# Two attention layers on one core: layer 0's maxima from VectorE to GpSimd, projections in pieces of 256 columns taken in two rounds, and GpSimd's side pieces only where VectorE has its own

## The chip, the cores and the metric

The kernel runs on one core of one Trainium2 chip. The core has five engines with instruction queues of their own: TensorE (PE; its weight loads are listed apart as PEld), VectorE (DVE), ScalarE (ACT), GpSimd (POOL) and SyncE (SP), which here only issues DMAs. The metric is the time of one execution on the device, in microseconds (us), as the median of several runs. The profile is that of one further execution.

## The reference

The inputs are `x` (3327 x 128) and a 0/1 adjacency `adj` (3327 x 3327, ones on the diagonal). Two layers follow each other, each with a residual and a layer norm. Layer 0 is one graph attention over the 3327 nodes. Layer 1 reshapes q, k and v to (128, 3327, 8): it is 128 separate attentions over all 3327 x 3327 pairs, each with inner length 8, and the adjacency is added twice to the scores.

```python
# layer 0
H = X @ W.T + b;  s = H @ a_s;  r = H @ a_r
e = leaky_relu(A * s + A * r.T, 0.2)
att = softmax(where(A > 0, e, NEG), axis=1);  H_out = att @ H
x = layernorm(x + H_out)
# layer 1, d = 128, n = 3327, h = 8
q = (x @ Wq.T).reshape(d, n, h)      # k and v alike
a = einsum('dnh,dmh->dnm', q, k) * d ** -0.5 + adj + adj
a = softmax(a, axis=2)
out = einsum('dnm,dmh->dnh', a, v).reshape(n, h * d)
x = layernorm(x + out @ Wo.T)
```

## The kernel before, in words

**Layer 1 sets the frame.** The 128 attentions are taken four at a time: 32 *groups*. In each group the 3327 queries are cut into seven *blocks* of columns (six of 476, the last of 472), and in each block the 3327 keys into 26 *chunks* of 128 rows. The loop walks groups, blocks and then 26 *rounds* per block, numbered n = 0 to 25; a round computes the scores of two half-chunks (a half-chunk is one chunk for two of the four attentions, 128 x 952 values). Three chunks make a *stretch* of three rounds; the ninth stretch of a block has only two chunks and two rounds, n = 24 and 25.

In a round TensorE first writes the scores of the two half-chunks into PSUM (`scb`, L154). What follows depends on the chunk:

- Every third chunk (0, 3, 6 ... 24, called `times`): ScalarE takes the exponential straight from PSUM (L1136, 128 x 952), and GpSimd multiplies it by a factor made from the adjacency (L1137).
- The other chunks: VectorE adds the adjacency to the scores (L1139, 128 x 952), and ScalarE takes the exponential one or two rounds later, mostly for the whole chunk at once (L968, 128 x 1904; `late`, `exp_late`).

Four rounds after a chunk is complete (`LAG = 4`), `products` multiplies it on TensorE with the values and adds it to the block's sums (`av`, L938). TensorE works through its queue in order, so a product that waits holds back the scores behind it. After the last chunk VectorE copies the sums out (L948). In the first group the factors are not there yet: for each of its 63 stretches GpSimd makes one from the adjacency (`make_factor`, L782) and a DMA stores it for the later groups.

**Layer 0 and the projections are spread over the rounds as side work.** Only the first tile of 128 rows is computed ahead of the loop; the other 25 tiles (`layer0(t)`) are cut into pieces, which `work_tensor` and `work` place in the rounds. A tile of layer 0 needs, for each of 26 chunks of neighbours, a maximum of a row and a column vector (`weigh`, L310, 128 x 129), a product with the adjacency (`mask`, L319, three chunks at once, 128 x 384), and a matmul (`product`, through L243). Then come a chain of small VectorE operations, a transpose, and the projections to k, q and v: `project` computes 128 columns into a PSUM bank, `halves` writes them as an upper part `hi` (L405) and the remainder `lo` (L408), `values` copies v out (L429). VectorE also counts the adjacency's entries (`count`, L328), and finished tiles of layer 1 are projected and normalised by `result`.

Each piece has a kind: "p" for TensorE, "d" for VectorE, "m" for GpSimd, "x" for a load that takes no place. Two rows of pieces wait for places, `main` (products, chain, projections, results) and `aside` (maxima, masks, counts); each is taken strictly in its order. A "d" piece is allowed in ten rounds of a block, n = 0, 4, 7, 10, 13, 16, 19, 22, 24 and 25, one piece each (`lane`); these ten are called *places* below. A "p" piece is allowed at n = 3 and at the same rounds but 0. An "m" piece is allowed in every round, one each. In `work` the pieces come behind the round's own additions and multiplications on their engines.

A tile has to be ready 18 rounds before the end of the group ahead of its first reader (`OPEN`, `reads`). If it is not, `finish_to` issues what is missing at once, without regard to places.

Of the kernel before, what the change touches and what calls it, by code (L numbers as in the profile page):

```python
# [13 lines left out]
ALU = mybir.AluOpType  # L14
# [7 lines left out]
LOWEST = -3.0e38  # L22
# [25 lines left out]
def kernel(  # L48
# [27 lines left out]
    nc = tc.nc  # L76
# [75 lines left out]
    def special():  # L152
# [9 lines left out]
        with ExitStack() as sx, tc.manual_schedule(engines=ALL):  # L162
# [8 lines left out]
            T3 = P // 3 + 1  # L171
# [97 lines left out]
            def layer0(t, side=True, trow=None, bank=bank, held=None):  # L269
# [5 lines left out]
                s = {"a": {}, "w": {}}  # L275
# [25 lines left out]
                def weigh(n, c0, c1):  # L301
                    i0 = CH[n][0]
                    if c0 == i0:
                        s["w"][n] = bgw.tile([P, CW, 3 * T3], F32, name="w")
                    for i in range(c0, c1):
                        w, e = s["w"][n][:, i - i0, :r], er[:, i : i + 1]
                        if side:

                            w = s["w"][n][:, i - i0, :].rearrange("p (a b) -> p a b", b=T3)
                            nc.vector.tensor_scalar(w, s["t"][:, :, :T3], e, None, op0=ALU.max)  # L310
                        else:
                            nc.vector.scalar_tensor_tensor(
                                w, trow[:, :r], e, s["a"][n][:, i - i0, :r], op0=ALU.max, op1=ALU.mult
                            )

                def mask(n, c0, c1):
                    i0 = CH[n][0]
                    w = s["w"][n][:, c0 - i0 : c1 - i0, :r]
                    nc.gpsimd.tensor_tensor(w, w, s["a"][n][:, c0 - i0 : c1 - i0, :r], op=ALU.mult)  # L319

                def count(n, h, k):
                    c = CH[n][1] - CH[n][0]
                    c0, c1 = c * h // 3, c * (h + 1) // 3
                    if c1 > c0:
                        a = s["a"][n][:, c0:c1, :r]
                        z = bg1.tile([P, (CW + 2) // 3, P], BF16, name="dump")[:, : c1 - c0, :r]
                        at = 6 * n + 2 * h + k
                        nc.vector.tensor_scalar(  # L328
                            z, a, float(k), None, op0=ALU.is_equal, op1=ALU.add, accum_out=even[:, t, at : at + 1]
                        )  # L330
# [56 lines left out]
                chain += [("d", together(*root[10:], scale)), ("p", turn), ("d", keep_turned)]  # L387


                QW = 128 if side else 512  # L390

                def project(w, c):
                    s["b"] = bank()
                    (by_columns if side else whole)(
                        s["b"][:, :QW], s["xT"], w[:, c : c + QW], r, start=True, stop=True
                    )

                def halves(dst, c, scale):
                    if c % 512 == 0:
                        s["hi"] = bg2.tile([P, 512], F32R, name="hi")  # L400
                        s["lo"] = bg2.tile([P, 512], F32R, name="lo")
                    o = c % 512
                    hi, lo = s["hi"], s["lo"]
                    if side:
                        nc.vector.tensor_scalar(hi[:r, o : o + QW], s["b"][:r, :QW], scale, None, op0=ALU.mult)  # L405
                    else:
                        nc.scalar.mul(hi[:r, o : o + QW], s["b"][:r, :QW], scale)
                    nc.vector.scalar_tensor_tensor(  # L408
                        lo[:r, o : o + QW], s["b"][:r, :QW], scale, hi[:r, o : o + QW].bitcast(F32),
                        op0=ALU.mult, op1=ALU.subtract,  # L410
                    )
                    if o + QW == 512:
                        h0 = c // 512 * 4
                        for half, sb in ((0, hi), (1, lo)):
                            at = (h0 * 2 + half if dst is qT else half * H + h0) * G + t * P * D
                            for p0, p1 in _cut(r):
                                later = held.append if held is not None and dst is qT else issue
                                engine = nc.sync if later is issue else nc.scalar
                                later(
                                    lambda at=at, sb=sb, p0=p0, p1=p1, engine=engine: engine.dma_start(  # L420
                                        _ap(dst, at + p0 * D, [[D, p1 - p0], [2 * G if dst is qT else G, 4], [1, D]]),
                                        sb[p0:p1].bitcast(F32).rearrange("p (h c) -> p h c", c=D),
                                    )
                                )
# [18 lines left out]
                for w, dst, sc in ((wk, kT, 1.0), (wq, qT, half_scale)):  # L443
                    for c in range(0, H * D, QW):
                        chain += [
                            ("p", lambda w=w, c=c: project(w, c)),
                            ("d", lambda dst=dst, c=c, sc=sc: halves(dst, c, sc)),
                        ]
                for c in range(0, H * D, QW):
                    chain += [("p", lambda c=c: project(wv, c)), ("d", lambda c=c: values(c))]  # L450
# [1 line left out]
                main, aside = [("x", load)], [("r", load_row)] if side else []  # L452
# [10 lines left out]
                for n, (i0, i1) in enumerate(CH):  # L463

                    aside.append(("n", ("P", q0 + n - 2, 0)))
                    for c0 in range(i0, i1, 3):
                        c1 = min(c0 + 3, i1)
                        aside.append(("d", lambda n=n, c0=c0, c1=min(c0 + 2, c1): weigh(n, c0, c1)))
                        if c0 + 2 < c1:
                            aside.append(("d", lambda n=n, c0=c0 + 2, c1=c1: weigh(n, c0, c1)))  # L470
                        if side:
                            aside.append(("m", lambda n=n, c0=c0, c1=c1: mask(n, c0, c1)))
                    aside.append(("t", ("W", q0 + n)))
                    c = [("d", lambda n=n, h=h, k=k: count(n, h, k)) for h in range(3) for k in range(2)]
                    counts.append(c)
                    main.append(("n", ("W", q0 + n, 3)))
                    if i1 == NT:
                        main.append(("m", biased))
                    main += [("p", lambda i=i: product(i)) for i in range(i0, i1)] + [("t", ("P", q0 + n))]
                    aside.append(counts[-1])  # L480
# [446 lines left out]
            NR = len(rounds)  # L927
# [56 lines left out]
            def lane(kind, n):  # L984
                middle = n % 3 == 1 and 4 <= n < NR - 2
                if kind == "p":
                    return int(middle or n == 3 or n >= NR - 2)
                return int(middle or n == 0 or n >= NR - 2)

            made = [layer0(t) for t in range(1, NT)]  # L990
# [2 lines left out]
            aside = []  # L993
# [25 lines left out]
            side = {"main": [], "aside": aside, "since": {"main": 0, "aside": 0}, "read": -2}  # L1019
# [27 lines left out]
            def run(row, now):  # L1047
                side[row].pop(0)[1]()
                side["since"][row] = now
# [6 lines left out]
                    run("main", now)  # L1056

            def work(now, n):
                room, pool = lane("d", n), 1
                for row in ("main", "aside"):  # L1060
                    while True:
                        kind = head(row, now)
                        if kind == "x":
                            pass
                        elif kind == "d" and room:
                            room -= 1
                            if row == "main":
                                side["read"] = now
                        elif kind == "m" and pool:
                            pool -= 1  # L1070
                        else:
                            break
                        run(row, now)
# [21 lines left out]
            for g in range(NG):  # L1095
                k4, v4, _ = group
                for b in range(NBLK):
                    s = Block()
                    s.g, s.b, s.q4, s.k4, s.v4, s.left, s.e, added = g, b, queries[0], k4, v4, NT, {}, {}
                    w = s.w = exact[b][2]  # L1100
                    for n, rnd in enumerate(rounds):
                        at = b * NR + n
                        if n in starts:
                            m = (g * NBLK + b) * NST + starts[n]
# [16 lines left out]
                        sc = []  # L1121
# [18 lines left out]
                        now = g * total + at  # L1140
# [403 lines left out]
```

## Time and profile before

| | |
|---|---|
| median of 3 runs | 10001.89 us (9998.2 to 10005.2) |
| the profiled execution's own time | 10004.91 us |
| its span | 10003.1 us |
| ACT busy | 9892.4 us (99%) |
| PE busy | 9461.4 us (95%) |
| DVE busy | 9334.1 us (93%) |
| POOL busy | 9201.7 us (92%) |
| first to last exponential of layer 1 | 65.9 to 9977.8 us |

The span leaves out 1.8 us of the profiled execution's time. Busy times are unions of the instructions' intervals. A duration in a row runs from an instruction's start to its end, and on DVE, ACT and POOL two neighbours overlap by 0.03 to 0.2 us when neither waits, so that the sum of the durations is above the busy time, and what one more instruction takes from its engine is somewhat less than its duration. "Idle before" is the time in which the engine stood still ahead of an instruction, with what ended it.

### The profile page before, as it was taken

The page shows a single profiled execution, that of the slowest core. Times are in us where ns is not written, and L with a number is a line of the kernel's source. Part 1 is how long each engine was busy: PE and PEld are TensorE (multiplying, and loading weights), DVE is VectorE, ACT ScalarE, POOL GpSimd, SP SyncE. Part 2 cuts the span into 40 slices and gives each one's busy share as a digit, 9 for nine tenths or more (in the row PEclk, how much of TensorE's full clock was granted, in tenths as well). Part 3 has the DMA queues.
Part 4 walks back from the last instruction along what each step waited for, and adds up shares of the span by engine and source line. Part 5 has one row for each costly group of instructions (what it writes and reads, how often), then busy time and mean ns, then how long its engine had stood idle before and what let it go on. Part 6 is the DMA issues. An engine that isn't in the chain of part 4 may idle for free.

```text
span 10003.1 us, 212173 instructions
## 1 busy us (share of the span) xinstructions
PE 9461.4 (95%) x81923; PEld 3078.5 (31%) x81923; DVE 9334.1 (93%) x11592; ACT 9892.4 (99%) x8352; POOL 9201.7 (92%) x4416
## 2 busy tenths in 40 slices
PE   7999999999999999999999999999999999999998
PEld 2233333333233333323333332333332333332222
DVE  7999999999999999999999999999999999999998
ACT  7999999999999999999999999999999999999998
POOL 7999999999999999999999999999999999999998
PEclk9999999999999999999999999999999999999999
DMA  7665666655656656656566665566665566656554
GB/s 200 200 176 169 177 172 177 178 167 174 177 165 175 182 161 178 177 169 176 165 173 174 181 179 164 163 178 179 177 174 168 164 179 177 175 161 171 167 168 125
DMA packets 1383200, 1728.31 MB, mean 173 GB/s; under 512 B 347463, under 2 KB 1370657, under 8 KB 1378079
## 3 DMA queue, kind: packets, MB, share of 16 engines
q1 hardware_dynamic: 1371828, 1712.03, 60.1%
q8 instruction: 644, 10.55, 0.4%
q10 hardware_dynamic: 10347, 2.61, 0.1%
q14 instruction: 381, 3.12, 0.1%
HBM read 1610.23 MB, written 103.93 MB: 171 GB/s over the span
## 4 chain that ended last, share of the span: by engine, by line
ACT 40%; PE 24%; POOL 16%; issue 11%; DVE 6%; DMA 2%; SPq 1%; POOLq 0%; ACTq 0%; DVEq 0%
ACT e L968 25%; POOL e L1137 16%; ACT e L1136 15%; PE scb L154 12%; PE av L938 11%; DVE e L1139 4%; PE bank L243 1%; DVE o L948 1%; DVE lo L408 0%; DMA q4b<-qT 0%; POOL w L319 0%; DMA at<-ftd 0%; DVE hi L405 0%; DMA k4b<-kT 0%; DVE w L310 0%
## 5 line engine op out<-in xcount | busy, mean ns | idle before, releaser
L1137 POOL TENSOR_TENSOR e<-e,at 128x952 f32<-128x952 f32 (+1 forms) x4032 | 8956.7, 2237 | 718.9 <-ACT e L1136 641.7
L1139 DVE TENSOR_TENSOR e<-scb,at 128x952 f32<-128x952 f32 (+1 forms) x7616 | 8420.0, 1143 | 579.3 <-PE scb L154 477.8
L968 ACT ACTIVATE e<-e 128x1904 f32<-128x1904 f32 (+2 forms) x4256 | 7104.0, 1678 | 2.0 <-DVE e L1139 1.6
L938 PE MATMUL av<-e,v4b 128*32 128x476 f32 x46592 | 5917.6, 572 | 60.6 <-DVE o L948 41.9
L154 PE MATMUL scb<-q4b,k4b 32*128 32x476 f32 (+1 forms) x23296 | 3749.2, 486 | 442.8 <-ACT e L1136 370.8
L1136 ACT ACTIVATE e<-scb 128x952 f32<-128x952 f32 (+1 forms) x4032 | 4078.6, 1012 | 57.5 <-PE scb L154 33.8
L154 PEld LDWEIGHTS scb<-q4b,k4b 32*128 32x128 f32 (+1 forms) x23296 | 1764.2, 189 | 5371.8 <-ACT e L1136 3489.9
L938 PEld LDWEIGHTS av<-e,v4b 128*32 128x32 f32 x46592 | 1059.2, 108 | 1140.0 <-issue 933.0
L243 PE MATMUL bank<-hsb,w 128*32 128x129 f32 (+1 forms) x5200 | 277.8, 285 | 0.0
L328 DVE TENSOR_SCALAR_CACHE_REDUCE dump<-a 128x384 bf16<-128x384 f32 (+2 forms) x468 | 247.1, 528 | 0.6
L319 POOL TENSOR_TENSOR w<-w,a 128x384 f32<-128x384 f32 (+3 forms) x225 | 207.7, 923 | 0.1
L310 DVE TENSOR_SCALAR w<-trow,er 128x129 f32<-128x129 f32 x650 | 201.1, 338 | 0.0
L948 DVE COPY o<-av 128x476 f32<-128x476 f32 (+1 forms) x224 | 145.9, 651 | 8.1 <-PE av L938 7.2
L243 PEld LDWEIGHTS bank<-hsb,w 128*32 128x32 f32 (+1 forms) x5200 | 102.4, 108 | 148.0 <-issue 148.0
L408 DVE SCALAR_TENSOR_TENSOR lo<-bank,hi 128x128 fp32r<-128x128 f32 (+1 forms) x400 | 116.5, 291 | 13.8
L405 DVE TENSOR_SCALAR hi<-bank 128x128 fp32r<-128x128 f32 (+1 forms) x400 | 112.0, 280 | 0.0
L243 PE MATMUL bank<-wv,x1T 128*32 128x128 f32 x1600 | 85.6, 286 | 3.9 <-DVE vb L429 3.9
L243 PE MATMUL bank<-wq,x1T 128*32 128x128 f32 x1600 | 85.4, 285 | 0.0
L243 PE MATMUL bank<-wk,x1T 128*32 128x128 f32 x1600 | 85.4, 285 | 0.0
L243 PE MATMUL bank<-wo,ot 128*32 128x128 f32 x1600 | 85.2, 285 | 0.0
L429 DVE COPY vb<-bank 128x128 f32<-128x128 f32 (+1 forms) x200 | 56.1, 281 | 5.8 <-PE bank L243 5.8
L503 PE MATMUL bank<-ident,o 128*128 128x128 f32 x225 | 52.0, 304 | 0.0
(123 smaller groups left out, 659.7 us busy)
## 6 DMA issues: line engine op xcount, KB each, us to landing
at<-in_adjT_dram SPq DMA_DIRECT2D x1536, 476.0 KB
at<-ftd SPq DMA_DIRECT2D x1674, 238.0 KB
at<-in_adjT_dram SPq DMA_DIRECT2D x256, 472.0 KB
at<-ftd SPq DMA_DIRECT2D x279, 236.0 KB
k4b<-kT SPq DMA_DIRECT2D x128, 415.9 KB
q4b<-qT SPq DMA_DIRECT2D x1528, 29.8 KB
at<-in_adjT_dram SPq DMA_DIRECT2D x186, 208.2 KB
a<-in_adjT_dram SPq DMA_DIRECT2D x50, 504.0 KB
```

What stands on the lines that cost most here:

```text
L154: nc.tensor.matmul(dst, k4[32 * j : 32 * j + H4, first_key(i) : first_key(i) + 2 * r - 1 : 2], q4[32 * j : 32 * j + H4, :nb], start=True, ...
L243: nc.tensor.matmul(dst[c0:c1], w[:, c0:c1], mov, **kw)
L310: nc.vector.tensor_scalar(w, s["t"][:, :, :T3], e, None, op0=ALU.max)
L319: nc.gpsimd.tensor_tensor(w, w, s["a"][n][:, c0 - i0 : c1 - i0, :r], op=ALU.mult)
L328: nc.vector.tensor_scalar(z, a, float(k), None, op0=ALU.is_equal, op1=ALU.add, accum_out=even[:, t, at : at + 1])
L408: nc.vector.scalar_tensor_tensor(lo[:r, o : o + QW], s["b"][:r, :QW], scale, hi[:r, o : o + QW].bitcast(F32), op0=ALU.mult, op1=ALU.subtract,)
L938: nc.tensor.matmul(s.av[32 * j : 32 * j + 32, : s.w], s.v4[:r, j, i * H1 : i * H1 + 32], e[:r, j, : s.w], start=(s.left == NT - 1), stop=( ...
L948: nc.vector.tensor_copy(o4[:, :w], s.av[:, :w])
L968: nc.scalar.activation(e, e, AF.Exp, scale=2.0)
L1136: nc.scalar.activation(eh, z[:r, :, :w], AF.Exp, scale=2.0)
L1137: nc.gpsimd.tensor_tensor(eh, eh, ah, op=ALU.mult)
L1139: nc.vector.tensor_tensor(eh, z[:r, :, :w], ah, op=ALU.add)
```

## The change

Four things are changed together.

1. `weigh` of the 25 side tiles runs on GpSimd instead of VectorE. It is the same maximum, written as a minimum with 3e38 followed by a maximum with the per-partition value. It is taken for three chunks in one "m" piece instead of two "d" pieces of two and one chunk.
2. GpSimd's "m" pieces (maxima, masks, and one bias addition a tile) are allowed only at the ten places of the "d" pieces, one each, no longer in every round.
3. `project` computes 256 columns at once instead of 128, so a tile has 12 projections instead of 24.
4. `halves` is split into `high`, a "d" piece, and `low`, a piece of a new kind "l" that has rounds of its own: n = 0, 1, 25 and every round with n % 3 = 2.

```diff
 # weigh, side tiles
-    nc.vector.tensor_scalar(w, s["t"][:, :, :T3], e, None, op0=ALU.max)
+    nc.gpsimd.tensor_scalar(w, s["t"][:, :, :T3], -LOWEST, e, op0=ALU.min, op1=ALU.max)
...
-                QW = 128 if side else 512
+                QW = 256 if side else 512
...
-                def halves(dst, c, scale):
+                def high(c, scale):
...
+                def low(dst, c, scale):
...
-                            ("d", lambda dst=dst, c=c, sc=sc: halves(dst, c, sc)),
+                            ("d", lambda c=c, sc=sc: high(c, sc)),
+                            ("l", lambda dst=dst, c=c, sc=sc: low(dst, c, sc)),
...
-                        aside.append(("d", lambda n=n, c0=c0, c1=min(c0 + 2, c1): weigh(n, c0, c1)))
-                        if c0 + 2 < c1:
-                            aside.append(("d", lambda n=n, c0=c0 + 2, c1=c1: weigh(n, c0, c1)))
-                        if side:
-                            aside.append(("m", lambda n=n, c0=c0, c1=c1: mask(n, c0, c1)))
+                        aside.append(("m", lambda n=n, c0=c0, c1=c1: weigh(n, c0, c1)))
+                        aside.append(("m", lambda n=n, c0=c0, c1=c1: mask(n, c0, c1)))
...
 def lane(kind, n):
+                if kind == "l":
+                    return int(n < 2 or n % 3 == 2 or n == NR - 1)
...
 def work(now, n):
-                room, pool = lane("d", n), 1
+                room, low, pool = lane("d", n), lane("l", n), lane("m", n)
...
+                        elif kind == "l" and low:
+                            low -= 1
+                            side["read"] = now
```

More of the change, by code (lines that the diff above doesn't have):

```diff
@@ L401, in halves @@
                         s["lo"] = bg2.tile([P, 512], F32R, name="lo")
-                    o = c % 512
-                    hi, lo = s["hi"], s["lo"]
+                    o, hi = c % 512, s["hi"]
                     if side:
@@ L407, in halves @@
                         nc.scalar.mul(hi[:r, o : o + QW], s["b"][:r, :QW], scale)
+                def low(dst, c, scale):
+                    o = c % 512
+                    hi, lo = s["hi"], s["lo"]
                     nc.vector.scalar_tensor_tensor(
```

## The prediction

> **What bounds the kernel now.** I read first the page's busy times and costliest groups, then the engines' busy time in stretches cut at the edges of groups, then the time lines of ScalarE and GpSimd where ScalarE stands still, and last the prices of the side pieces with shapes kept apart.
>
> ```profile
> PE 9461.4 (95%) x81923; PEld 3078.5 (31%) x81923; DVE 9334.1 (93%) x11592; ACT 9892.4 (99%) x8352; POOL 9201.7 (92%) x4416
> ...
> L1137 POOL TENSOR_TENSOR e<-e,at 128x952 f32<-128x952 f32 (+1 forms) x4032 | 8956.7, 2237 | 718.9 <-ACT e L1136 641.7
> L1139 DVE TENSOR_TENSOR e<-scb,at 128x952 f32<-128x952 f32 (+1 forms) x7616 | 8420.0, 1143 | 579.3 <-PE scb L154 477.8
> L968 ACT ACTIVATE e<-e 128x1904 f32<-128x1904 f32 (+2 forms) x4256 | 7104.0, 1678 | 2.0 <-DVE e L1139 1.6
> ...
> L1136 ACT ACTIVATE e<-scb 128x952 f32<-128x952 f32 (+1 forms) x4032 | 4078.6, 1012 | 57.5 <-PE scb L154 33.8
> ```
>
> ScalarE is the wall: it waited 2.0 us in all for VectorE's additions and 57.5 us ahead of L1136. The same by groups (group 0, group 1, group 2, group 8, group 31; the columns are us, then busy of PE, PEld, DVE, ACT, POOL):
>
> ```profile
> 65.90:402.80 336.90, 303.30 (x2569) 94.26 (x2573) 295.92 (x380) 311.56 (x260) 322.57 (x201) 0.95 0.74 209
> 402.80:717.30 314.50, 297.48 (x2645) 97.36 (x2641) 296.50 (x383) 308.93 (x261) 291.28 (x142) 0.99 0.61 176
> 717.30:1025.70 308.40, 294.42 (x2613) 96.63 (x2609) 293.77 (x374) 308.40 (x260) 289.30 (x141) 1.00 0.61 173
> 2568.00:2876.40 308.40, 293.62 (x2383) 90.60 (x2379) 285.12 (x331) 308.40 (x261) 282.75 (x131) 1.00 0.61 171
> 9662.60:9977.80 315.20, 295.83 (x2343) 87.93 (x2335) 281.34 (x315) 309.68 (x260) 284.17 (x132) 0.99 0.48 144
> ```
>
> A group takes 308.4 us with ScalarE busy throughout, whatever VectorE does beside it. Only groups 0, 1 and 31 are longer, by 28.5, 6.1 and 6.8: 41 us is all that any relief could win. In group 0 POOL is busy for 322.6 of 336.9; it makes the 63 factors there.
>
> ScalarE's time line shows where groups 0 and 1 lose most, and how much lateness of GpSimd is free:
>
> ```profile
> 371.93 0.96 ACT L1136 ACTIVATE e<-scb 128x944 f32<-128x944 f32 x1 [5.22 <-PE scb L154]
> ...
> 402.66 1.02 ACT L1136 ACTIVATE e<-scb 128x952 f32<-128x952 f32 x1
> ...
> 412.44 0.96 ACT L1136 ACTIVATE e<-scb 128x952 f32<-128x952 f32 x1 [1.13 <-PE scb L154]
> ...
> 448.01 1.03 ACT L1136 ACTIVATE e<-scb 128x952 f32<-128x952 f32 x1
> ...
> 686.51 0.96 ACT L1136 ACTIVATE e<-scb 128x944 f32<-128x944 f32 x1 [4.24 <-PE scb L154]
> ```
> ```profile
> 404.26 13.17 POOL L1137 TENSOR_TENSOR e<-e,at 128x944 f32<-128x944 f32 x6
> ...
> 451.43 0.92 POOL L319 TENSOR_TENSOR w<-w,a 128x384 f32<-128x384 f32 x1
> 452.30 11.02 POOL L1137 TENSOR_TENSOR e<-e,at 128x952 f32<-128x952 f32 x5
> ```
>
> The 5.22 and 4.24 are `finish_to`: tiles 1 and 2 are late by eleven pieces, and TensorE and VectorE go through the last projections in turn. The others are edges between blocks. ScalarE ended chunk 0's second half at 403.68 (402.66 + 1.02); GpSimd, with six multiplications from 404.26 at 2.19 each, began it third, at 408.6: 4.9 us late, and ScalarE then stood for 1.13. A block later it ended at 449.04 and GpSimd began at 452.30: 3.3 late, and nothing stood. So about **3.7 us of lateness at the edge is free** (4.9 less 1.13), and what is above it is paid.
>
> **The change part by part.** The prices:
>
> ```profile
> L310 DVE TENSOR_SCALAR w<-trow,er 128x129 f32<-128x129 f32 x650 | 201.1, 338 | 0.0
> L319 POOL TENSOR_TENSOR w<-w,a 128x384 f32<-128x384 f32 x192 | 183.9, 958 | 0.1
> L408 DVE SCALAR_TENSOR_TENSOR lo<-bank,hi 128x128 fp32r<-128x128 f32 x384 | 111.8, 291 | 13.3
> L405 DVE TENSOR_SCALAR hi<-bank 128x128 fp32r<-128x128 f32 x384 | 107.5, 280 | 0.0
> ...
> L782 POOL TENSOR_SCALAR at<-at 128x476 f32<-128x476 f32 x54 | 32.0, 592 | 4.6
> ...
> L512 DVE TENSOR_TENSOR ot<-bank,x1T 128x256 f32<-128x256 f32 x75 | 31.0, 414 | 0.0
> ...
> masks.py:199 POOL TENSOR_SCALAR_AFFINE_SELECT ident<-ident 128x128 f32<-128x128 f32 x1 | 0.3, 297 | 0.0
> ```
>
> *VectorE loses work, worth nothing.* 201.1 us of maxima go. Per tile 8 `hi` of 280 ns become 4, and 8 `lo` of 291 become 4; a 256-column piece is about 0.41 (the 414 of L512). ScalarE waited 2.0 us for VectorE in all, so at most 2 us comes back; I take 0. The reverse: a stretch has 5.06 us (two exponentials of each kind, 2.53 a pair on the time line). Four additions, 1.06 apart, take 4.22, and `hi` and `lo` now 0.33 each by the same overlap: 4.89, 0.17 to spare. The 0.65 copy of L948 uses that up once a block; VectorE's waits for scores (0.26 each, 477.8 in all) cover it. Without that cover 0.1 us in each of 25 x 8 projecting stretches would be 20. I take 0.
>
> *TensorE.* 24 projections of a tile become 12 twice as wide. Eight passes of 128 columns take 0.43 us and of 476 columns 1.00 (time line), so one takes about 0.64: 12 x 0.64 for 24 x 0.43, off the path. `hi` and `lo` hold the bank over one more round; the next projection comes a round later still. The stores of q and k stay as many on SP, issued with `low`. I take 0.
>
> *`finish_to` ends: -9.5.* The order of the changed program issues nothing out of place: tile 1 is ready in round 140 of the 164 it has, tile 2 in group 1 at round 108. A tile needs 45 VectorE pieces (8 of them in rounds of their own) for 66. The 5.22 and 4.24 go.
>
> *GpSimd gets 650 maxima.* No row shows this operation on POOL. From below: a 128-wide memset (210 ns, L700 in the groups by form), from above the two-input 128-wide addition of L346 (466). Nearest is the one-input operation of the same width, 297; L782 less 347 elements at 1 ns gives 245. I take 0.30, and 0.25 of the engine's time, since neighbours overlap by 0.05 (five multiplications of 2.237 in 11.02). The ends are 0.15 and 0.42. So a piece of three maxima takes 0.75 and a mask 0.91.
>
> A stretch has 5.06 us for two multiplications of 2.19: 0.68 to spare. One piece at each place costs 0.75 or 0.91, and the pieces now come back to back, six in a row and more: +0.3 of lateness every two stretches, harmless. The edge is not. The short stretch gives 3.5 us for 4.4 of work; without any piece GpSimd is 1.5 late at the edge (ScalarE's half ends at 9575.73, GpSimd's begins at 9577.2). Places 24, 25 and 0 lie right there: three pieces add 2.4 (0.75 + 0.91 + 0.75) or 2.6, which makes 3.9 to 4.1, and what the run before left 0.1 to 0.9 more. Behind a late multiplication waits `products` on TensorE, behind that the scores of n = 6, behind those ScalarE.
>
> - *Groups 2 to 22:* in the changed program's order 36 edges carry three pieces (157 none, 16 one). At 0.2 to 0.4 over the free 3.7 and on average 0.2 carried: 36 x 0.5 = **+18**. Before, no edge there stood.
> - *Group 0*, where GpSimd is full anyhow: 44 maxima x 0.25 and two masks more, 12.8, of which some runs on into group 1: **+11**.
> - *Group 1:* three full edges behind a group that ends late: **+4**.
>
> Sum: -9.5 + 18 + 11 + 4 = +23.5. The judge pieces that make group 31 longer move to groups 23 and 24 at the same price. The profiled execution's 10004.9 becomes 10028.4; it lay 3.0 above the median of the runs, so **10025**.
>
> At other prices of a maximum (about nine are in play per edge): 0.15 gives +1 (edges 2, group 0 +7, group 1 +2), 0.20 +10 (8, 9, 2.5), 0.30 +43 (34, 13, 5), 0.42 about +100.
>
> The Trainium skill speaks against the move: GPSIMD Engine Reference, section Engine selection, gives elementwise work to VectorE, GPSIMD being some 2x slower with two inputs and roughly at line rate with one. The row agrees for two inputs (958 ns for 384 elements); none here shows the one-input maximum. By 1.03 cycles an element at 1.2 GHz, which the page gives for short loop bodies (section Elementwise — side-by-side cycle accounting), 129 elements are 0.11 us, and with the 0.18 that L782 has over its 476 elements I estimate 0.29, +21 in the sum.
>
> **The rivals.**
>
> - *Not slower: the maximum is cheap.* It decides below 0.24 of engine time: then few edges exceed 3.7, and the lost `finish_to` pays for group 0. Time 10003 (at 0.15) to 10020. For it: the 145 that a memset takes behind a neighbour, 245 from L782. Against it: 297 at the same width, a scalar read per partition, and an access of 3 x 43. Chance 0.40.
> - *Two-input price.* Each maximum at 0.42 of the engine: about 10100, for the same edges overflow by over 2 us. For it: L346. Against it: one tensor input. Chance 0.10.
> - *VectorE's pairs.* `hi` and `lo` overrun the stretch: +20 on top, 10045. For it: 0.17 spare. Against it: 2.0 us of waiting in the whole profile. Chance 0.08.
> - *A gain of over 20* would need half of the 41 us of lost time; GpSimd's overload in group 0 can only grow. Chance 0.02.
>
> **How the numbers follow.** A measurement of this kernel can tell 0.2%, 20 us, from no change. My forecast has 0.40, and the cases above it 0.18 more: slower 0.57, same 0.41, faster 0.02. Low is the cheap maximum, 10003; high 0.38 a maximum, 10085. The forecast's own range is 10012 to 10050.
>
> **What would show it.** L310 on POOL near 0.30 us; no 5 us idle of ScalarE in groups 0 and 1; GpSimd over 3.7 us late at full edges and ScalarE waiting for scores there by about 0.5; group 0 longer than 337, later groups without full edges still 308.4; VectorE's share down by some 2.5 points, worth nothing. Wrong I am if a maximum costs far from 0.25, or if a product that waits slows TensorE beyond the wait itself (its clock falls to 0.95 in group 0), which makes each edge dearer.

## The result

| | before | after |
|---|---|---|
| median | 10002.3 us (9998.2 to 10006.5, 6 runs) | 10095.44 us (10093.5 to 10099.1, 6 runs) |
| profiled execution, its own time | 10004.91 us | 10093.52 us |
| its span | 10003.1 us | 10091.7 us |

The ratio is 1.0093 with a 95% interval of 1.008 to 1.0106: slower, by 0.9%. The forecast was 10025 with a range of 10003 to 10085. The direction was right; the size lies outside the range, 70 us above the forecast.

The page of the changed kernel: busy times, then the chain that ended last, then the groups (busy us, mean ns of one, idle time before them and its releaser). L1136, L1137, L1139, L968 and L938 of before are now L1142, L1143, L1145, L969 and L939.

```profile
PE 9455.4 (94%) x79523; PEld 2957.4 (29%) x79523; DVE 9116.4 (90%) x10442; ACT 9905.8 (98%) x8352; POOL 9402.8 (93%) x5066
...
ACT 33%; PE 25%; POOL 23%; issue 12%; DVE 5%; DMA 2%; SPq 0%; POOLq 0%; ACTq 0%; DVEq 0%
...
L1145 DVE TENSOR_TENSOR e<-scb,at 128x952 f32<-128x952 f32 (+1 forms) x7616 | 8423.2, 1143 | 892.9 <-PE scb L154 742.3
L969 ACT ACTIVATE e<-e 128x1904 f32<-128x1904 f32 (+2 forms) x4256 | 7063.4, 1668 | 4.9 <-DVE e L1145 3.6
L939 PE MATMUL av<-e,v4b 128*32 128x476 f32 x46592 | 5937.4, 575 | 150.9 <-POOL e L1143 108.4
L1142 ACT ACTIVATE e<-scb 128x952 f32<-128x952 f32 (+1 forms) x4032 | 4036.9, 1001 | 130.4 <-PE scb L154 104.5
...
L310 POOL TENSOR_SCALAR w<-trow,er 128x129 f32<-128x129 f32 x650 | 234.3, 388 | 1.5
L319 POOL TENSOR_TENSOR w<-w,a 128x384 f32<-128x384 f32 (+3 forms) x225 | 210.5, 936 | 0.2
```

VectorE's share fell from 93% to 90% and GpSimd's rose from 92% to 93%; ScalarE waits 130.4 us instead of 57.5 for scores. It waits no more for VectorE than it did (4.9 and 2.0 us). The new row is on TensorE: its products (L939) stand 108.4 us for GpSimd's multiplications, 18.6 us before. A maximum lasts 388 ns on GpSimd.

The groups of the changed kernel in the same columns as before: us, busy time of PE, PEld, DVE, ACT and POOL, granted clock, DMA share, GB/s. These are groups 0, 1, 2, 8, 17 and 31, each cut at its first exponential from PSUM:

```profile
64.43:411.05 346.62, 303.60 (x2529) 92.54 (x2529) 285.68 (x331) 311.66 (x258) 334.02 (x239) 0.93 0.71 202
411.05:732.01 320.96, 299.33 (x2625) 96.75 (x2625) 289.94 (x349) 309.85 (x261) 310.21 (x196) 0.98 0.60 172
732.01:1045.82 313.81, 298.14 (x2591) 95.17 (x2589) 293.43 (x362) 309.65 (x260) 299.73 (x170) 0.99 0.63 180
2600.61:2910.54 309.93, 294.61 (x2566) 94.58 (x2562) 286.26 (x333) 308.64 (x260) 293.67 (x164) 1.00 0.60 170
5412.63:5730.56 317.93, 300.87 (x2544) 94.52 (x2546) 291.12 (x355) 309.65 (x260) 300.19 (x171) 0.98 0.62 177
9756.02:10063.64 307.62, 285.23 (x2261) 82.71 (x2259) 271.50 (x268) 307.62 (x260) 279.39 (x126) 1.00 0.49 146
```

Cut by that rule, before has 335.0 us in group 0, 314.5 in group 1, 308.4 in an undisturbed group and 314.3 in group 31. So the loss is spread over all groups that still have layer 0's tiles, and group 31, which has none, is as short as a group can be.

One block edge shows how a group loses. This is block 2 of group 17, the dearest edge of groups 2 to 24: first GpSimd's time line, then those of ScalarE and TensorE together (start, us, engine, instruction, in brackets the idle time before it and its releaser):

```profile
5507.11 0.97 POOL L319 TENSOR_TENSOR w<-w,a 128x384 f32<-128x384 f32 x1
5508.03 2.24 POOL L1143 TENSOR_TENSOR e<-e,at 128x952 f32<-128x952 f32 x1
5510.25 1.06 POOL L310 TENSOR_SCALAR w<-trow,er 128x129 f32<-128x129 f32 x3
5511.28 2.23 POOL L1143 TENSOR_TENSOR e<-e,at 128x952 f32<-128x952 f32 x1
5513.47 0.92 POOL L319 TENSOR_TENSOR w<-w,a 128x384 f32<-128x384 f32 x1
5514.34 10.90 POOL L1143 TENSOR_TENSOR e<-e,at 128x952 f32<-128x952 f32 x5
```
```profile
5507.60 1.01 ACT L1142 ACTIVATE e<-scb 128x952 f32<-128x952 f32 x1
...
5512.87 1.00 PE L939 MATMUL av<-e,v4b 128*32 128x476 f32 x8 [0.29 <-DVE o L949]
...
5516.60 1.81 PE L939 MATMUL av<-e,v4b 128*32 128x476 f32 x8 [2.18 <-POOL e L1143]
5518.34 0.77 PE L154 MATMUL scb<-q4b,k4b 32*128 32x476 f32 x4
...
5519.21 0.96 ACT L1142 ACTIVATE e<-scb 128x952 f32<-128x952 f32 x1 [2.97 <-PE scb L154]
```

A mask, three maxima and a mask lie at the places n = 24, 25 and 0. ScalarE ended chunk 0's second half at 5508.61; GpSimd began it at 5514.34, 5.7 us late. The product of that chunk waited 2.18 us for it, the scores of n = 6 stood behind that product, and ScalarE stood 2.97 us. That is more than the wait itself, because TensorE came back slow: eight passes took 1.81 us instead of 1.00 and the scores 0.77 instead of 0.49. The granted clock (last but two in the columns of the groups) over the stretches before, at and after the wait; the 0.87 of the middle row means that it fell to half within the wait, at about 5515.4:

```profile
5500.00:5512.00 12.00, 11.57 (x104) 3.69 (x100) 10.96 (x16) 12.00 (x14) 12.00 (x12) 1.00 0.55 174
5512.00:5516.60 4.60, 2.04 (x17) 0.67 (x17) 4.53 (x8) 4.24 (x4) 4.60 (x4) 0.87 0.44 140
5516.60:5520.80 4.20, 4.20 (x24) 0.71 (x24) 1.17 (x2) 1.59 (x2) 4.20 (x2) 0.50 0.59 173
```

### The profile page after: what moved, and what is told of

Read it like the earlier page. It is cut to its first block, busy times and chain, and to the rows that moved or that the text cites. A ratio compares the mean times of both kernels' runs of the same rounds, so it can differ in the third digit from the quotient of the medians.

```text
span 10091.7 us, 206814 instructions
## 1 busy us (share of the span) xinstructions
PE 9455.4 (94%) x79523; PEld 2957.4 (29%) x79523; DVE 9116.4 (90%) x10442; ACT 9905.8 (98%) x8352; POOL 9402.8 (93%) x5066
## 4 chain that ended last, share of the span: by engine, by line
ACT 33%; PE 25%; POOL 23%; issue 12%; DVE 5%; DMA 2%; SPq 0%; POOLq 0%; ACTq 0%; DVEq 0%
ACT e L969 22%; POOL e L1143 20%; PE av L939 12%; ACT e L1142 11%; PE scb L154 10%; DVE e L1145 3%; PE bank L243 1%; POOL w L310 1%; POOL w L319 1%; DVE o L949 1%; DMA at<-in_adjT_dram 1%; DMA q4b<-qT 0%; DVE dump L328 0%; DMA a<-in_adjT_dram 0%; DVE hi L404 0%
## 5 line engine op out<-in xcount | busy, mean ns | idle before, releaser
L1143 POOL TENSOR_TENSOR e<-e,at 128x952 f32<-128x952 f32 (+1 forms) x4032 | 8948.0, 2242 | 605.4 <-ACT e L1142 550.1
L1145 DVE TENSOR_TENSOR e<-scb,at 128x952 f32<-128x952 f32 (+1 forms) x7616 | 8423.2, 1143 | 892.9 <-PE scb L154 742.3
L969 ACT ACTIVATE e<-e 128x1904 f32<-128x1904 f32 (+2 forms) x4256 | 7063.4, 1668 | 4.9 <-DVE e L1145 3.6
L939 PE MATMUL av<-e,v4b 128*32 128x476 f32 x46592 | 5937.4, 575 | 150.9 <-POOL e L1143 108.4
L1142 ACT ACTIVATE e<-scb 128x952 f32<-128x952 f32 (+1 forms) x4032 | 4036.9, 1001 | 130.4 <-PE scb L154 104.5
L154 PEld LDWEIGHTS scb<-q4b,k4b 32*128 32x128 f32 (+1 forms) x23296 | 1696.5, 189 | 5441.8 <-ACT e L1142 3277.1
L939 PEld LDWEIGHTS av<-e,v4b 128*32 128x32 f32 x46592 | 1041.2, 108 | 1352.6 <-issue 925.9
L310 POOL TENSOR_SCALAR w<-trow,er 128x129 f32<-128x129 f32 x650 | 234.3, 388 | 1.5
L411 DVE SCALAR_TENSOR_TENSOR lo<-bank,hi 128x256 fp32r<-128x256 f32 (+1 forms) x200 | 83.2, 416 | 0.7
L404 DVE TENSOR_SCALAR hi<-bank 128x256 fp32r<-128x256 f32 (+1 forms) x200 | 83.1, 415 | 0.0
L243 PE MATMUL bank<-wk,x1T 128*32 128x256 f32 x800 | 64.3, 393 | 0.0
L243 PE MATMUL bank<-wq,x1T 128*32 128x256 f32 x800 | 63.9, 391 | 0.0
L243 PE MATMUL bank<-wv,x1T 128*32 128x256 f32 x800 | 63.9, 391 | 0.0
L243 PEld LDWEIGHTS bank<-wo,ot 128*32 128x32 f32 x1600 | 31.5, 108 | 45.5 <-issue 45.5
```

The source lines that it names most:

```text
L154: nc.tensor.matmul(dst, k4[32 * j : 32 * j + H4, first_key(i) : first_key(i) + 2 * r - 1 : 2], q4[32 * j : 32 * j + H4, :nb], start=True, ...
L243: nc.tensor.matmul(dst[c0:c1], w[:, c0:c1], mov, **kw)
L310: nc.gpsimd.tensor_scalar(w, s["t"][:, :, :T3], -LOWEST, e, op0=ALU.min, op1=ALU.max)
L411: nc.vector.scalar_tensor_tensor(lo[:r, o : o + QW], s["b"][:r, :QW], scale, hi[:r, o : o + QW].bitcast(F32), op0=ALU.mult, op1=ALU.subtract,)
L939: nc.tensor.matmul(s.av[32 * j : 32 * j + 32, : s.w], s.v4[:r, j, i * H1 : i * H1 + 32], e[:r, j, : s.w], start=(s.left == NT - 1), stop=( ...
L969: nc.scalar.activation(e, e, AF.Exp, scale=2.0)
```

## The experiments

The theory: the loss is GpSimd's maxima. They make GpSimd late at block edges; above 3.7 us of lateness a product waits, and ScalarE with it. The rivals: VectorE's pieces (`high` and `low`) or the wide projections cost; or GpSimd's load as such costs, wherever its pieces lie. What the expectations call queue arithmetic replays GpSimd's queue on paper: ScalarE's undisturbed times, 2.19 us a multiplication, the pieces at their places with a price, and every edge above 3.7 us late delays all that follows. What they call excess is ScalarE's time from the end of one exponential to the end of the next, less what that takes back to back, summed.

### Parts 3 and 4 alone: the maxima back on VectorE

```diff
-    nc.gpsimd.tensor_scalar(w, s["t"][:, :, :T3], -LOWEST, e, op0=ALU.min, op1=ALU.max)
+    nc.vector.tensor_scalar(w, s["t"][:, :, :T3], e, None, op0=ALU.max)
...
-    aside.append(("m", lambda n=n, c0=c0, c1=c1: weigh(n, c0, c1)))
+    aside.append(("d", lambda n=n, c0=c0, c1=min(c0 + 2, c1): weigh(n, c0, c1)))
+    if c0 + 2 < c1:
+        aside.append(("d", lambda n=n, c0=c0 + 2, c1=c1: weigh(n, c0, c1)))
...
 def lane(kind, n):
+                if kind == "m":
+                    return 1
```

> The maxima go back to VectorE (one input, per-row scalar, in its places as before); the 256-column projections, the upper and lower parts in two rounds stay; GpSimd keeps the masks, one piece in any round. Theory (the loss is GpSimd's maxima, 388 ns a row and about 0.347 us from one start to the next, which hold back the products of chunk 0 at block edges): the edges are as before, and the two waits of ScalarE at forced rounds (5.22 and 4.24 us) are gone, so about 9.5 us below the kernel before: 9993, range 9985 to 10000; ScalarE's excess in the loop near 30 us, where the kernel before has 39.6 and the changed kernel 129.5. Rival (the pair of projection pieces, or the wider projections, cost ScalarE or TensorE in their rounds): 10005 to 10025, with new waits of ScalarE in the rounds that hold upper and lower parts.

Measured: 10002.58 us (11 runs) beside 10002.61 for the kernel before; ratio 1.0, interval 0.9991 to 1.0009. The edit puts back parts 1 and 2 of the change, for GpSimd's masks are again allowed in any round. So parts 3 and 4 cost nothing without the other two, and the whole loss of 93 us goes with the maxima and their places. But the saving of 9.5 us did not show either: the time lies between the theory's range and the rival's. Its groups 0 and 1, and its row of ScalarE's waits for scores:

```profile
65.68:398.45 332.77, 299.49 (x2521) 92.24 (x2521) 293.24 (x367) 310.04 (x257) 320.94 (x200) 0.95 0.72 210
398.45:710.51 312.06, 297.97 (x2573) 94.64 (x2577) 295.90 (x374) 308.89 (x260) 294.40 (x145) 0.99 0.61 178
```
```profile
L1147 ACT ACTIVATE e<-scb 128x952 f32<-128x952 f32 (+1 forms) x4032 | 4055.7, 1006 | 56.6 <-PE scb L154 32.3 <-DMA v4b<-vd 22.3 <-issue 0.2
```

The stalls of 5.22 and 4.24 us are gone, but groups 0 and 1 are only 2.2 and 2.4 us shorter: the pieces that `finish_to` had issued in a lump now lie at edges that had been free of them (the wait at n = 6 of the first block of group 1 is 2.7 us where it was 1.1). Ten block edges of groups 5 to 21 also have a wait of 0.21 us at n = 3. All ten have the same order on VectorE, a count at n = 24, an upper and a lower part at n = 25, a count at n = 0; the first two lines here are that round's pieces, the next ones the additions and the count:

```profile
3002.89 0.41 DVE L404 TENSOR_SCALAR hi<-bank 128x256 fp32r<-128x256 f32 x1
3003.34 0.42 DVE L411 SCALAR_TENSOR_TENSOR lo<-bank,hi 128x256 fp32r<-128x256 f32 x1
3003.68 1.14 DVE L1150 TENSOR_TENSOR e<-scb,at 128x952 f32<-128x952 f32 x1
3004.74 0.54 DVE L328 TENSOR_SCALAR_CACHE_REDUCE dump<-a 128x384 bf16<-128x384 f32 x1
```

This profiled execution was 7 us above its own median; 5.7 us of it stand in one place, at the start of group 18, for which I have no cause.

### Upper and lower parts kept apart at the edge

```diff
 # the kernel with the maxima back on VectorE
-    return int(n < 2 or n % 3 == 2 or n == NR - 1)
+    return int(n % 3 == 2)
```

> The run with the maxima back on VectorE, with one more change: lower parts only in every third round (n = 2, 5, ..., 23), no longer at n = 0, 1 and 25, so that no upper and lower part share round 25 between two other pieces of VectorE. The order of the layer's rows finishes in the same rounds. Theory (in the run with the maxima back, upper and lower part at n = 25 between pieces at n = 24 and n = 0 make ScalarE wait 0.21 us at n = 3; ten such places gave 2.1 us, and groups 0 and 1 held 4.9 us more than the kernel before without its two forced stalls): those ten waits go, and some of the 4.9: 9994 to 10000. Rival (the saving of the forced rounds is lost elsewhere, as by the 256-column matmuls themselves): 10001 to 10005.

Measured: 9999.08 us (11 runs) beside 10003.1; ratio 0.9998, interval 0.9989 to 1.0007. The profiled executions are further apart, 9998.21 and 10004.91.

```profile
L1147 ACT ACTIVATE e<-scb 128x952 f32<-128x952 f32 (+1 forms) x4032 | 4057.5, 1006 | 49.1 <-PE scb L154 26.1 <-DMA v4b<-vd 22.1
```

That is inside the theory's 9994 to 10000. The waits at n = 3 in groups 2 to 24 fall from 4.4 us (2.1 at the ten pairs, 1.6 at the start of group 18) to 0.2. So VectorE's pairs did cost what the trace shows at n = 3. This is the only version with a median below the kernel before, by 4 us, and the runs do not tell that from no change.

### The place of GpSimd's pieces: none at the edges, anywhere, and spread

```diff
 # "none at the edges"
 def lane(kind, n):
+                if kind == "m":
+                    return int(middle)
 # "anywhere", instead of the two lines above
+                if kind == "m":
+                    return 1
 # "spread": none at the edges, and in work()
+                if now >= 2 * total and n not in (4, 10, 16, 22):
+                    pool = 0
```

> GpSimd's pieces (maxima and masks) only at the middle places (every third of n = 4 to 22), none at n = 24, 25 and 0; everything else as in the changed kernel, so GpSimd does as many instructions in the whole. Theory (place: three pieces in a row about a block edge, 4.2 to 5.7 us late where 3.7 is free): the edge stalls of groups 2 to 22 go, those of groups 0 and 1 partly stay (about 27 and 7 us of excess): 10017 to 10030. Rival (load: GpSimd is 93% busy and its sum decides): no change from the changed kernel, 10085 to 10100.

> GpSimd's pieces, maxima and masks, in any round (one a round), as the kernel before places its masks; maxima stay on GpSimd. Theory of the edges: runs of pieces sit wherever the loads let them, more of them in a row, so more stalls than in the changed kernel: queue arithmetic gives 25 us more excess than at the changed kernel's places (154 against 129), and 60 if stalls cost more than the lateness above 3.7: 10120 to 10170. Rival (load alone): as the changed kernel, 10085 to 10100. Rival (the fixed places are themselves the loss, since they put pieces on edges): below the changed kernel, 10040 to 10080.

> The run with no pieces of GpSimd at the edges, with one more change: from group 2 on GpSimd takes a piece only at n = 4, 10, 16 and 22, so at most four in a block where it had seven; the same instructions, spread over more blocks. Theory (GpSimd has about 4 us free in a block of 44.3; seven pieces of 0.7 to 1.04 us pass that and the lateness is carried into the block's edge; four do not): the score waits at n = 6 (6.9 us in groups 2 to 24 of that run) and n = 15 to 24 (3.5 us) go, those at n = 3 that belong to VectorE's pairs (4.7 us) stay: 10 us less than that run's 10040, so 10025 to 10034. Rival (moving the maxima to GpSimd costs by its load wherever they are): no change, 10037 to 10043.

Measured: none at the edges 10040.5 (ratio 1.0036, 1.0023 to 1.005), anywhere 10212.4 (1.0205, 1.019 to 1.0221), spread 10019.0 (1.0016, 1.0007 to 1.0025). The row of ScalarE's waits for scores in the three, in this order:

```profile
L1144 ACT ACTIVATE e<-scb 128x952 f32<-128x952 f32 (+1 forms) x4032 | 4046.5, 1004 | 73.7 <-PE scb L154 46.2 <-DMA v4b<-vd 22.4
```
```profile
L1144 ACT ACTIVATE e<-scb 128x952 f32<-128x952 f32 (+1 forms) x4032 | 4029.7, 999 | 234.1 <-PE scb L154 207.7 <-DMA v4b<-vd 22.2 <-ACT e L969 0.3
```
```profile
L1146 ACT ACTIVATE e<-scb 128x952 f32<-128x952 f32 (+1 forms) x4032 | 4056.7, 1006 | 64.1 <-PE scb L154 38.1 <-DMA v4b<-vd 22.2 <-POOL e L1147 0.3
```

All three and the changed kernel run the same 650 maxima and 225 masks on GpSimd, and their times lie 193 us apart. So the load does not decide; how many pieces come together does. "Anywhere" lies above its range of 10120 to 10170, "spread" below its 10025 to 10034. With pieces in any round, runs of them make GpSimd late at n = 9 to 24 as well. With four a block, groups 2 to 22 are 7.9 us above the kernel before (sum of their lengths), where the changed kernel has 75.3. "None at the edges" lies 10 us above its range: 13.7 us of waits at n = 2 and 3 in groups 2 to 24 were not in it. 4.7 of them are the pairs of VectorE; the other 9 lie mostly at the starts of groups, and what makes them was not tried.

### Narrow projections again

```diff
-                QW = 256 if side else 512
+                QW = 128 if side else 512
...
-                            ("d", lambda c=c, sc=sc: high(c, sc)),
-                            ("l", lambda dst=dst, c=c, sc=sc: low(dst, c, sc)),
+                            ("d", lambda dst=dst, c=c, sc=sc: (high(c, sc), low(dst, c, sc))),
```

> Projections of 128 columns again, upper and lower parts in one piece at one place; the maxima stay on GpSimd at the places of VectorE's pieces. Theory (only the maxima cost; a pending list that runs later changes which blocks hold pieces): one forced wait of about 5 us comes back, the edges stay, queue arithmetic gives 60 us of excess against 92 for the changed kernel by the same arithmetic: 10037 to 10065. Rival (the separated wide pieces are a large part of the loss): under 10030. Rival (they are worth much where GpSimd is late): above 10100.

Measured: 10048.07 us (ratio 1.0044, 1.0029 to 1.006), within the theory's range. With the maxima on GpSimd, the wide projections in two rounds are worth 47 us of loss; with the maxima on VectorE they were worth nothing. They cost nothing themselves. By the order of the instructions they let a tile finish in fewer rounds, so that the maxima follow each other more closely: in the changed kernel 47 block edges of groups 2 to 24 are over 3.9 us late, 36 of them with three pieces of GpSimd, with the narrow projections 25, 12 of them with three.

### The price of a maximum

Four kernels keep every place of the changed kernel and change only what a piece of maxima costs. *Flat*: the thresholds lie in one run instead of three of 43. *Constant*: 0.5 instead of the row's threshold. *One operation*: the maximum without the minimum ahead of it. *Sums*: one two-input addition for the whole piece.

```diff
 # flat
-    s["t"] = bg2.tile([P, 3, T3 + 1], F32, name="trow")
+    s["t"] = bg2.tile([P, 3 * T3], F32, name="trow")
 # constant
-    nc.gpsimd.tensor_scalar(w, s["t"][:, :, :T3], -LOWEST, e, op0=ALU.min, op1=ALU.max)
+    nc.gpsimd.tensor_scalar(w, s["t"][:, :, :T3], -LOWEST, 0.5, op0=ALU.min, op1=ALU.max)
 # one operation
+    nc.gpsimd.tensor_scalar(w, s["t"][:, :, :T3], e, None, op0=ALU.max)
 # sums (thresholds flat)
+    both = [P, c1 - c0, 3 * T3]
+    nc.gpsimd.tensor_tensor(
+        s["w"][n][:, c0 - i0 : c1 - i0, :],
+        s["t"].unsqueeze(1).to_broadcast(both),
+        er[:, c0:c1].unsqueeze(2).to_broadcast(both),
+        op=ALU.add,
+    )
```

> The changed kernel with the row of thresholds laid out as 387 numbers in one run, so that a maximum reads and writes 129 contiguous numbers instead of 3 pieces of 43. Theory (the price of a maximum sets the loss; the 388 ns are 338 ns of VectorE's same shape, whose reading is also in three pieces, plus GpSimd's start): if the layout is part of the price, 20 to 60 ns less per maximum, and by the queue arithmetic 0.4 to 0.9 us of time per ns: 10045 to 10085. If the layout costs nothing: 388 ns again and 10090 to 10100. Rival (the time does not hang on the price): a lower price at the same time.

> The changed kernel with a constant in place of the threshold that each row brings (one number per partition): the second operand of each maximum is 0.5, so the weights are not those of the reference; every instruction, place and size else is the same. If the operand by partition is the price: 40 to 120 ns less per maximum and, at 0.4 to 0.9 us of time per ns, 10000 to 10080. If it is not: 388 ns and 10090 to 10100. Rival (the time does not hang on the price): a lower price at the same time.

> The changed kernel with each maximum as one operation (maximum with the row's threshold) in place of two (minimum with a large constant, then the maximum); the result is the same. In the changed kernel one maximum follows the next by 345 ns and a piece of three takes GpSimd 1.034 us; with a constant operand it was 357 ns and 1.217 us, and the time 41 us longer, 0.68 us for each ns of a third of a piece. Theory (the piece's time on GpSimd, from product to product, sets the loss): the second operation costs something, and each ns saved per maximum brings 0.68 us: 20 to 40 ns less gives 10068 to 10082; none less gives 10090 to 10100. Rival (the time does not follow the piece's time): no relation to it.

> The changed kernel with the thresholds' row flat and each piece as one two-input operation over 3 x 129 (or 2 x 129) numbers, of which both inputs are spread; it adds where the kernel takes maxima, so the weights are not those of the reference; places and counts of pieces are the same. The mask of 3 x 128 in the same form took 969 ns with about 919 from product to product, against 1034 for a piece of three maxima. Theory (the piece's time on GpSimd sets the loss, 0.68 us of time per ns of a third of a piece): a piece near 925 ns, 36 ns less per maximum, 10060 to 10080. Rival (the form or the number of instructions sets it, or the load alone): 10090 to 10100.

The row of the maxima, and a piece of three on GpSimd's time line with the multiplications around it; first the constant, then one operation, then the sums:

```profile
L310 POOL TENSOR_SCALAR w<-trow 128x129 f32<-128x129 f32 x650 | 191.6, 295 | 45.0
```
```profile
5435.21 2.22 POOL L1143 TENSOR_TENSOR e<-e,at 128x944 f32<-128x944 f32 x1 [0.22 <-ACT e L1142]
5437.51 1.01 POOL L310 TENSOR_SCALAR w<-trow 128x129 f32<-128x129 f32 x3
5438.60 4.39 POOL L1143 TENSOR_TENSOR e<-e,at 128x944 f32<-128x944 f32 x2
```
```profile
L310 POOL TENSOR_SCALAR w<-trow,er 128x129 f32<-128x129 f32 x650 | 386.2, 618 | 0.1
```
```profile
5413.98 1.76 POOL L310 TENSOR_SCALAR w<-trow,er 128x129 f32<-128x129 f32 x3
5415.72 4.40 POOL L1143 TENSOR_TENSOR e<-e,at 128x952 f32<-128x952 f32 x2
```
```profile
L307 POOL TENSOR_TENSOR w<-trow,er 128x387 f32<-128x387 f32 x200 | 169.3, 847 | 0.1
```
```profile
5406.95 2.23 POOL L1147 TENSOR_TENSOR e<-e,at 128x952 f32<-128x952 f32 x1 [0.24 <-ACT e L1146]
5409.15 0.83 POOL L307 TENSOR_TENSOR w<-trow,er 128x387 f32<-128x387 f32 x1
5409.94 4.42 POOL L1147 TENSOR_TENSOR e<-e,at 128x952 f32<-128x952 f32 x2
```

The second column below is the median time from the end of the multiplication before a piece of three to the start of the one after it; two multiplications without a piece overlap by 0.044 us, so a third of (gap + 0.044) is what a maximum takes from the engine.

| kernel | gap, us | a maximum takes, ns | its duration, ns | time, us | ratio to before |
|---|---|---|---|---|---|
| sums | 0.743 | 262 | (847 for three) | 10049.87 | 1.0044 (1.0027 to 1.006) |
| changed kernel | 0.992 | 345 | 388 | 10095.44 | 1.0093 (1.008 to 1.0106) |
| flat | 0.999 | 348 | 383 | 10100.3 | 1.0097 (1.0081 to 1.0112) |
| constant | 1.173 | 406 | 295 | 10136.87 | 1.0134 (1.0118 to 1.0149) |
| one operation | 1.705 | 583 | 618 | 10264.41 | 1.0259 (1.0242 to 1.0276) |

Each kernel's time above the kernel before in its own runs (43.4, 93.1, 97.2, 133.8 and 258.0 us) follows the engine time in order and nearly in a line: 0.60 us per ns of a maximum from the sums to the changed kernel, 0.67 from there to the constant, 0.70 on to one operation. It does not follow the duration: the constant's instructions are 93 ns shorter than the changed kernel's and its time is 41 us longer. Its row says why: it has 45.0 us of idle time ahead of it, and the time line has 0.08 us between the multiplication and the piece, where the changed kernel's instructions overlap (2.24 us from 5508.03, and the next one at 5510.25).

What a change of form does to the price was guessed badly. The flat layout changed nothing, one of its two cases; the constant and the single operation went neither of the ways expected, and the sums saved 83 ns instead of 36. That the price sets the time held each time.

## Why the prediction was wrong

*The step that failed: "I take 0.30, and 0.25 of the engine's time".* The overlap of 0.05 was right (388 against 345). The duration was not: 388 ns, where I took the nearest one-input row of the same width, 297 (a mask pattern without an operand per row). By the prediction's own scale (+43 at 0.30, about +100 at 0.42) the measured 0.345 makes +64 instead of +23.5, 41 of the 70 us missed. The runs agree: the sums kernel is nearly the forecast's case, with 262 ns, and lies 43 us above the kernel before, the changed kernel 93; 50 us for the price. Of the 29 us that the price leaves, about 5 are the `finish_to` term below; most of the rest is the edges.

*The edges were too cheap as well.* I had 36 edges at 0.5 us for groups 2 to 22. The count was right: the trace has 36 edges with three pieces in groups 2 to 24, all over 3.9 us late (the 157 and 16 beside it run on to group 31). The price of an edge was not: near the forecast's price of a maximum (sums) these 36 cost 0.73 us each, at 345 ns 1.60. Eleven more edges of the changed kernel are late with one piece or none, by what GpSimd carried into them; I had called the lateness of a run of pieces harmless. In all, over 3.9 us late were 37 edges with the sums and 47 in the changed kernel, and ScalarE's excess at rounds 5 to 9 was 30.8 and 71.1 us. Why an edge costs more than its lateness shows in a table over those edges. Lateness is the start of GpSimd's second multiplication of chunk 0 less the end of ScalarE's exponential; the entries are the mean excess in us and, in brackets, the number of edges.

| lateness, us | below 3.4 | 3.9 to 4.5 | 4.5 to 5.0 | 5.0 to 5.5 | 5.5 to 6.5 | 6.5 to 9 |
|---|---|---|---|---|---|---|
| before | 0.00 (161) | | | | | |
| sums | 0.03 (120) | 0.48 (21) | 1.05 (16) | | | |
| changed kernel | 0.03 (110) | 0.58 (10) | 1.20 (19) | 1.74 (10) | 2.73 (8) | |
| constant | 0.03 (110) | 0.56 (6) | 1.20 (13) | 2.35 (19) | 2.69 (13) | |
| one operation | 0.03 (104) | 0.38 (2) | 0.85 (7) | 2.10 (2) | 3.26 (23) | 4.26 (18) |

The free lateness of 3.7 us, read from two edges of the kernel before, holds in all five kernels. Above it the excess is the lateness less 3.7 up to 5 us, and up to 0.8 us more than that beyond. In the changed kernel 58.6 us of lateness above 3.65 became 71.1 us of excess, some 3 of them at edges that were less than 3.4 late.

What an edge costs beyond its lateness is TensorE's clock. At 34 of the changed kernel's 47 late edges the granted clock stayed up, and there the excess is the lateness less 3.7 to within 0.1 us, at each of them. At the other 13 it fell to half, and the excess is 0.9 us more on average, 11.9 us in all. So the mechanism that the prediction named only as a way to be wrong was real, but it is 11.9 of the 71.1 us; the rest is plain lateness.

When the clock falls is not a matter of the wait's length alone. In all traces here the granted clock changes only at the bounds of equal steps of 3.41 us. In groups 2 to 24 of the changed kernel it fell 13 times, each time after a step in which TensorE had stood still for 1.37 us or more; 13 of the 20 steps with over 1.3 us of standing still were followed by half the clock, and none of the others. A product's wait of 2.13 us that ended at 2031.65 lay across two steps and left the clock at 1.00 (first two rows); a wait of 1.47 us that lay within one step was followed by 0.50 (last two). There the product that had waited still ran at full speed, and the passes behind it were slow.

```profile
2027.00:2030.40 3.40, 2.52 (x28) 0.83 (x24) 3.33 (x6) 3.40 (x4) 3.40 (x3) 1.00 0.63 205
2030.40:2033.80 3.40, 2.15 (x20) 0.51 (x20) 1.90 (x3) 1.53 (x2) 3.40 (x3) 1.00 0.33 81
3675.60:3679.00 3.40, 1.93 (x20) 0.67 (x16) 2.29 (x3) 2.42 (x2) 3.40 (x2) 1.00 0.20 27
3679.00:3682.40 3.40, 3.40 (x28) 1.08 (x28) 1.90 (x2) 3.17 (x3) 3.40 (x4) 0.50 0.62 203
```

The Trainium skill has the rule behind these rows, in "TensorE: Matmul & The Clock Gate", Part 1: the array's clock falls to half after an idle window of about 3.4 us. The clock of 0.50 and the step of 3.41 us agree. But the step need not be idle throughout: here 1.37 us of standing still in one was enough, though 1.88 us in another was not.

*By groups*, the changed kernel less the kernel with the maxima back on VectorE: group 0 +13.8 us (forecast +11), group 1 +8.9 (+4), groups 2 to 22 +64.9 (+18), or 71 without the unexplained 5.7 of the other. The judge pieces (the tests of the sums and counts) moved to groups 23 and 24 as said, and group 31 is short.

*"`finish_to` ends: -9.5"* was half right. The two stalls went, as the order of the instructions said; groups 0 and 1 became 4.6 us shorter, not 9.5, since the pieces cost something at the places that they took. With VectorE's lower parts moved off the edge it is 6.8 us. I had asked what the lump of pieces cost, and not what the same pieces cost where they would lie next.

*"VectorE loses work, worth nothing"* held: ScalarE waits 4.9 us for its additions, and groups 25 to 30 take 308.3 us as before. The count of pieces in that paragraph was wrong: the rows have 400 upper parts for 25 tiles, so 16 a tile became 8, not 8 became 4; no term of the sum hangs on it. The rival about VectorE's pairs was real but small: ten to some twenty edges at 0.21 us, not the 20 us it was priced at. *"TensorE: 0"* and the stores at 0 held as far as the runs show: nothing in the kernel with the maxima back stands for them.

*The two-input rival* (about 10100, chance 0.10) came closest to the time, in part by luck: its price of 0.42 was too high by about as much as its edges were too cheap. *The cheap maximum* (chance 0.40) has no support: no form that was run came below 262 ns.

*The rule quoted ahead* from "GPSIMD Engine Reference", section Engine selection, that one-input work runs roughly at line rate on GPSIMD, depends on the form here: the same 129 numbers take 338 ns on VectorE as one operation, and on GpSimd 618 as one, far from the same rate, and 388 as two, 15% more. The estimate of 0.29 from that page's cycles was too low for either.

## What to carry to other kernels

Price an operation that no row shows by what it takes from one start to the next, and where the two nearest rows differ by a factor of 1.6 carry the dearer one through the sum before choosing: each ns here was worth about 0.6 us. An engine with 4 us free in a block of 44 hides side work only if no more than that comes between two points where someone waits for it: with the same 875 instructions on GpSimd the kernel is 93 us above the kernel before as the change places them, and 16 us with at most four pieces a block. And when a lump of work is to be dissolved, price it at the places where it goes.

## What had not been expected of the hardware

- On GpSimd the maximum of 128 x 129 numbers with a value per partition lasted 618 ns as one operation, and 388 ns with a minimum ahead of it in the same instruction. The kernel's odd-looking minimum with 3e38 is worth 238 ns per instruction (345 against 583 of engine time).
- With a constant for that value the instruction became shorter (295 ns) and yet took more of the engine (406 ns), since it no longer overlapped with its neighbours.
- One two-input addition over 387 numbers took 847 ns, less than three one-input instructions over 129 each (1.03 us).
- TensorE's granted clock changed only at the bounds of steps of 3.41 us. It fell to half after a step in which TensorE had stood still for only 1.37 to 2.19 us (13 times in groups 2 to 24 of the changed kernel), and stayed there for one step or two.
